# Sixteen-head attentions: scores computed twice, four heads at a time, in place of transposed probabilities

## The chip, the cores and the metric

The kernel runs as one program on one core of a Trainium2 chip. The metric is the device time of one execution in microseconds; three runs of the kernel before gave 1425.77, 1425.83 and 1428.66 us. The engines of the core have short names in what follows: PE multiplies matrices, and the loading of its stationary operand has a row of its own, PEld; DVE, ACT and POOL work on tiles element by element; SP issues transfers (DMA). SBUF is the memory in which tiles lie, PSUM the small memory of eight banks that PE writes its products to, 512 float32 numbers in each of 128 partitions to a bank.

## The reference, cut to what matters

A decoder of two layers works on x of 8 batches x 256 tokens x 256 features, all in float32. After each of six sublayers the input is added and the sum normalised. The sublayers are a state-space mixer, a cross-attention, a mixture of experts, a self-attention with rotated queries and keys, a second cross-attention, and a self-attention whose tokens are split in two sets. Only the fourth and the sixth are touched. Both have 16 heads of 16 features.

```python
def _L1_attn_ref(x, w_qkv, w_out, b_out):          # "rotary"
    q, k, v = ...                                   # 16 heads of 16
    q = _apply_rope(q, cos, sin); k = _apply_rope(k, cos, sin)
    attn = softmax(einsum('bhsd,bhtd->bhst', q, k) * SCALE)
    out = einsum('bhst,bhtd->bhsd', attn, v)
    return einsum('bsd,ed->bse', out, w_out) + b_out

def _L1_ffn_ref(x, g_info, W_qkv, W_proj, b_proj):  # "split"
    pos = sim > 0.9                 # a sign for each token, from its normed queries
    def masked_attn(tok_mask):      # keys: 5 registers and the tokens of one sign
        l = where(key_mask, q * scale @ k, -inf)
        return softmax(l) @ v
    reg_out = (x_pos[:, :REG] + x_neg[:, :REG]) * 0.5
    tok_out = where(pos, x_pos[:, REG:], x_neg[:, REG:])
    return concatenate([reg_out, tok_out]) @ W_proj + b_proj
```

So a query of 256 tokens sees 256 keys; in the split attention only those of its own sign, and the registers attend twice.

## The kernel before

Both attentions use one class, `Heads16`, which runs them in 32 steps, four to a batch. The class `Rotary` and the function `split` give it queries, keys and a term to add, and the work that stands between its parts.

Queries and keys lie feature by token: a partition is a feature, and 32 partitions hold a pair of heads. The keys exist in two copies, each with one head of the pair set to zero (`kps`, made by POOL with the constant `slot`, L1189 and L1391). So a matmul over 32 partitions gives one head's scores, and both copies side by side give two heads' scores in 512 columns.

Step i has half of the heads, c, and one block of 128 queries, qb. `scores` (L1023) makes four matmuls, one for each 32 partitions, into two pairs of PSUM banks. A query is a partition here and a key is a column. For each of eight heads DVE adds the term, negates and takes the minimum in one instruction (L1032, 128x256), which also copies the scores to SBUF; ACT takes the exponential with that minimum as its bias and accumulates the sum (L1039).

The products need the keys on the partitions, so `turn` transposes the exponentials of the step before: 16 transposes on PE (L1054) into two pairs of banks, and a copy of each pair to SBUF, one on DVE and one on ACT (L1057). Every second step `products` (L1069) makes 16 matmuls for one c, into the bank "op". The sums are inverted, widened by POOL (L1084), turned by four transposes (L1091), copied (L1096) and multiplied with the products (L1100). `out` is the output projection (L1107).

`work(b, k, place)` puts other work at three places of a step k: projections of the next batch (L988, copied out by DVE or ACT), values (L998), the end of the batch before (normalisation in L104 to L117), and in split the registers (L1430 scores, L1450 turn, L1461 products) and the mask. The term of split is made by POOL and DVE from the signs (L1412, L1415); the signs of batch 0 are spread by a matmul, those of later ones by a DMA from a DRAM tile `sgd` (L1576 writes it, L1408 reads).

A scheduler orders instructions; `issue_after` adds edges that hold an engine's own program order. These put a step's scores first, its `work` and turns after DVE's last minimum was issued. PSUM is divided by tags: three pairs of banks "sc" (scores and turned exponentials), one bank "mm" (all small matmuls), one bank "op".

## Time and profile before

| | us |
|---|---|
| median of three runs | 1425.83 |
| profiled execution, its own time | 1423.73 |
| its span, first to last instruction | 1421.9 |
| rotary attention: first scores start | 711.2 |
| rotary attention: last scores start, last output projection starts | 908.6, 921.5 |
| split attention: first scores start | 1203.9 |
| split attention: last scores start, last output projection starts | 1395.9, 1410.3 |
| busy: PE, DVE, ACT, POOL | 1358.5, 847.1, 651.6, 483.3 |

The two attentions take about 400 us of the 1422. The page gives busy time over the whole program, so a stage has to be read from windows that lie in it, the price of an operation from its group, and the order from the chain of waits. In a timeline row the first number is the start in us, the second the time. A group's row ends with busy us, mean ns of one instruction, and the idle time before them with what ended it. A float32 matmul has two records, each with a weight load of its own. Rows L1032 and L1039 have a second record for the accumulator's reading.

### The profile page before, as it was taken

The numbers are of one execution on the slowest core, as the hardware profiler recorded it, in microseconds if no ns is written. First come the engines' busy times: TensorE is split into PE (matmuls) and PEld (weight loads), VectorE is DVE, ScalarE is ACT, GpSimd is POOL, SyncE is SP. The second block draws the span as 40 slices with busy tenths as digits, with TensorE's granted clock in tenths as the row PEclk, the third lists the DMA queues.
The fourth block names the chain that finished last, engine by engine and source line by source line (L and its number), as shares of the span: only waits on it lengthen the run. The fifth ranks groups of instructions, "written<-read, shape, count | busy, mean of one in ns | idle before, by whom it ended". The sixth has DMA issues, their size and how long they took to land.

```text
span 1421.9 us, 21978 instructions
## 1 busy us (share of the span) xinstructions
PE 1358.5 (96%) x7946; PEld 947.0 (67%) x7946; DVE 847.1 (60%) x2306; ACT 651.6 (46%) x1612; POOL 483.3 (34%) x510
## 2 busy tenths in 40 slices
PE   8999999999999999999989999999999999899996
PEld 3455678888866666656656666577878777666554
DVE  3776465555643223324578888745556563887885
ACT  3455533333331022221178787643332323867884
POOL 0100012131200132236346666332334454465541
PEclk9999999999999999999999999999999999999999
DMA  8000053335240022242120000025231200000100
GB/s 279 3 1 0 1 161 95 105 91 162 93 192 0 24 74 89 79 142 66 34 82 2 1 1 1 1 86 161 75 95 60 90 7 9 16 16 24 24 16 16
DMA packets 71487, 87.97 MB, mean 62 GB/s; under 512 B 5588, under 2 KB 66164, under 8 KB 70868
## 3 DMA queue, kind: packets, MB, share of 16 engines
q1 hardware_dynamic: 67972, 77.26, 17.0%
q0 software_dynamic: 3408, 9.31, 2.3%
q8 instruction: 64, 1.05, 0.3%
q14 instruction: 43, 0.35, 0.1%
HBM read 57.03 MB, written 29.52 MB: 61 GB/s over the span
## 4 chain that ended last, share of the span: by engine, by line
PE 65%; DVE 12%; POOL 3%; issue 2%; ACT 2%; DMA 1%; POOLq 0%; DVEq 0%; ACTq 0%; SPq 0%
PE mm L521 9%; PE sc L476 8%; PE mm L779 7%; DVE p L1032 6%; PE mm L842 5%; PE op L1069 4%; PE ps_sc L1054 4%; PE ps_sc L1023 4%; PE tr L796 4%; PE tr L856 2%; PE sc L505 2%; PE sc L457 2%; PE sc L411 2%; PE sc L375 2%; PE ps_mm L988 1%
## 5 line engine op out<-in xcount | busy, mean ns | idle before, releaser
L1039 ACT ACTIVATE p<-p,nmx 128x256 f32<-128x256 f32 x512 | 252.9, 496 | 65.2 <-DVE nmx L1032 65.1
L496 POOL TENSOR_TENSOR p<-p,sm 128x616 f32<-128x616 f32 x60 | 72.7, 1217 | 245.1 <-DVE sm L493 218.5
L521 PE MATMUL mm<-Ub,pT 128*128 128x256 f32 (+1 forms) x640 | 144.6, 379 | 0.5 <-ACT pT L75 0.4
L476 PE MATMUL sc<-M,xT_s 128*128 128x308 f32 x512 | 139.0, 423 | 1.1 <-ACT pT L75 1.1
L1054 PE MATMUL ps_sc<-ident,p 128*128 128x128 f32 x1024 | 133.3, 278 | 6.5 <-DVE nmx L1032 4.8
L1054 PEld LDWEIGHTS ps_sc<-ident,p 128*128 128x128 f32 x1024 | 114.6, 142 | 33.3 <-issue 13.3
L521 PEld LDWEIGHTS mm<-Ub,pT 128*128 128x128 f32 (+1 forms) x640 | 120.8, 190 | 20.0 <-ACT pT L75 0.9
L476 PEld LDWEIGHTS sc<-M,xT_s 128*128 128x128 f32 x512 | 94.4, 188 | 35.3 <-ACT pT L75 2.1
L489 ACT ACTIVATE p<-p 128x616 f32<-128x616 f32 x64 | 45.9, 717 | 154.4 <-DVE p L485 132.7
L779 PE MATMUL mm<-xT_s,w 128*128 128x512 f32 x256 | 113.4, 595 | 2.2 <-DVE h L785 2.2
L1032 DVE CUSTOM_DVE_ANT_0 p<-ps_sc,zero 128x256 f32<-128x256 f32 x256 | 90.7, 421 | 27.3 <-PE ps_sc L1023 25.7
L1032 DVE CUSTOM_DVE_ANT_0 p<-ps_sc,term 128x256 f32<-128x256 f32 x256 | 90.7, 419 | 25.8 <-PE ps_sc L1023 25.7
L1039 ACT ACTIVATION_READ_ACCUMULATOR p<-p,nmx 128x1 f32 x512 | 95.9, 187 | 0.0
L816 POOL DMA_INDIRECT xb<-xd,token x39 | 37.3, 956 | 146.2 <-PE tr L823 81.0
L779 PEld LDWEIGHTS mm<-xT_s,w 128*128 128x128 f32 x256 | 47.8, 190 | 56.0 <-issue 52.6
L1057 DVE COPY pT<-ps_sc 128x1024 f32<-128x1024 f32 x64 | 77.6, 1213 | 3.0 <-PE ps_sc L1054 3.0
L483 DVE TENSOR_REDUCE nmx<-sc 128x8 f32<-128x616 f32 x64 | 51.1, 798 | 46.2 <-PE sc L476 46.2
L1057 ACT COPY pT<-ps_sc 128x1024 f32<-128x1024 f32 x64 | 63.7, 996 | 26.8 <-PE ps_sc L1054 26.7
L842 PE MATMUL mm<-wE,xbT 128*128 x156 | 73.5, 593 | 0.3 <-ACT xbT L828 0.3
L783 ACT ACTIVATE g<-mm 128x512 f32<-128x512 f32 x32 | 19.1, 597 | 100.8 <-PE mm L779 99.7
L492 DVE TENSOR_REDUCE sm<-p 128x8 f32<-128x616 f32 x64 | 50.6, 790 | 22.2 <-ACT p L489 21.8
L114 POOL TENSOR_SCALAR rstd<-mv 128x2 f32<-128x2 f32 x48 | 10.8, 225 | 155.2 <-DVE mv L112 154.6
(295 smaller groups left out, 2635.7 us busy)
## 6 DMA issues: line engine op xcount, KB each, us to landing
Ub<-ud SPq DMA_DIRECT2D x32, 512.0 KB
ud<-U SPq DMA_DIRECT2D x16, 616.0 KB
wE<-in_wE SPq DMA_DIRECT2D x4, 1536.0 KB
yd<-y SPq DMA_DIRECT2D x39, 128.0 KB
Ub<-ud SPq DMA_DIRECT2D x32, 104.0 KB
ud<-U SPq DMA_DIRECT2D x4, 608.0 KB
x_s<-in_x SPq DMA_DIRECT2D x8, 256.0 KB
w<-in_Wo SPq DMA_DIRECT2D x2, 1024.0 KB
```

The source lines that it names most:

```text
L476: nc.tensor.matmul(sc[:, a, : 4 * NCTX], xT_b[:, kc, j * P : (j + 1) * P], M[:, a * 4 : a * 4 + 4, kc, at : at + NCTX], start=kc == 0, sto ...
L496: engine.tensor_tensor(pv, pv, bcast(sm, 2, [P, 8, NCTX]), ALU.mult)
L521: nc.tensor.matmul(o[:, j * D : (j + 1) * D], pT[:n, c, j * P : (j + 1) * P],  Us[b][:n, g, c], start=g == 0 and j == 0 and c == 0, stop=g ...
L779: nc.tensor.matmul(ps, w[:, kc, cols], xT_s[:, kc, :], start=kc == 0, stop=kc == 1)
L796: nc.tensor.matmul(o[:, j * D : (j + 1) * D], hs[c][:, at : at + P], w3[:, c, :], start=c == 0, stop=c == 7,)
L842: nc.tensor.matmul(ps, xT[:, kc, :], column(j, kc * 512, 512), start=kc == 0, stop=kc == 1)
L1023: self.last_score = nc.tensor.matmul(scs[s // 2][:, s % 2, :], self.queries(b, c, s, qb), self.keys(b, c, s), start=True, stop=True, tile_ ...
L1032: self.last = nc.vector.tensor_tensor_reduce(out=p[:, h, :], in0=s4[:, h, :], in1=self.term(b, qb), scale=-1.0, scalar=3.0e38, op0=ALU.add ...
L1039: nc.scalar.activation(p[:, h, :], p[:, h, :], AF.Exp, bias=nmx[:, qb, n : n + 1], scale=-1.0, accum_out=sums[:, qb, n : n + 1],)
L1054: nc.tensor.transpose(tr[:, at : at + P], p[:, h, kb * P : (kb + 1) * P], ident)
L1057: (nc.scalar.copy if j else nc.vector.tensor_copy)(self.pT[b, c, j][:, :, :, qb * P : (qb + 1) * P], tr.rearrange("p (h k t) -> p h k t", ...
L1069: nc.tensor.matmul(self.op[b][s * 32 : (s + 1) * 32, c, :], va[:, kb, 8 * c + 2 * s + m, :], self.pT[b, c, s // 2][:, s % 2 * 2 + m, kb, : ...
```

## The change

A step now has four heads and all 256 queries, and computes their scores twice. All in `Heads16`:

- `scores` makes eight matmuls with 256 columns, the queries of both blocks against one copy of the keys. DVE takes plain maxima, four at a time in 128x1024 (L1038 of the changed kernel), negated, into one column in 32 of a tile that is zero elsewhere; the scores are not copied.
- `turn_maxima` turns that tile with two transposes (L1048): the maxima come out as one row in every 32 partitions. `shifted` adds them to the queries (rotary in one instruction with a mask, L1188; split L1403). The keys hold ones in that row, a feature of the other head's that is not used.
- `exponentials`, one step later, makes the scores again with the keys as the stationary operand (L1061), so that they come out turned and shifted, and ACT takes exponentials from PSUM straight to the tile that the products read (L1069, 128x1024).
- `products`, two steps later, makes eight matmuls (L1080). The values' tile has ones in its unused columns, so the sums come out with the products. ACT copies them to SBUF (L1087).
- The sums go by DMA to a packed tile (L1091, 64 pieces of 64 bytes), are inverted (L1098), go back by two DMAs (L1100), are spread over partitions by a shuffle (L1108), and multiplied (L1112), after a predicated copy that merges the two heads of a pair (L1109).

In split the mask is no longer a term added by DVE. Two rows of each 32 partitions hold the signs, marked by DMAs from `sgd` into queries and keys (`marked`, eight a batch), and the queries exist in two copies. The bank "op" is now handed out by `side()` for products, turned maxima, turned outputs and the registers' matmuls. Projections, values and output projections are split in halves (`halves`) that stand before and after the second scores, and their copies are on ACT. What was `work` is a table of events by step and place.

```diff
         def scores(self, i):
-            c, qb = divmod(k, 2)
+            c, m = divmod(k, 2)
             scs = [self.pair() for _ in range(2)]
-            for s in range(4):
-                self.last_score = nc.tensor.matmul(
-                    scs[s // 2][:, s % 2, :], self.queries(b, c, s, qb), self.keys(b, c, s),
-                    start=True, stop=True, tile_position=(s * 32, 0),
+            for qb in range(2):
+                for s in range(4):
+                    nc.tensor.matmul(
+                        scs[s // 2][:, s % 2, qb * SEQ : (qb + 1) * SEQ],
+                        self.queries(b, c, s, m)[:, qb * P : (qb + 1) * P],
+                        self.keys(b, c, s, m), start=True, stop=True, tile_position=(s * 32, 0),
+                    )
+            for j in range(2):
+                self.last = nc.vector.tensor_reduce(
+                    self.mx[m][:, :, 2 * j : 2 * j + 2, self.free[m]].rearrange("p q s -> p s q"),
+                    scs[j].rearrange("p s (q t) -> p s q t", q=2), AX.X, ALU.max, negate=True,
                 )
...
+        def turn_maxima(self, i):
+            ps = self.side()
+            for qb in range(2):
+                nc.tensor.transpose(
+                    ps[:, qb * P : (qb + 1) * P],
+                    self.mx[m][:, qb].rearrange("p s x -> p (s x)"), ident,
+                )
+            qs = self.qs[i] = self.c2.tile([P, SEQ], F32, tag="qs", name="qs")
+            self.shifted(b, c, m, qs, ps[:, :SEQ])
+
+        def exponentials(self, i):
+            scs, qs = [self.pair() for _ in range(2)], self.qs.pop(i)
+            for kb in range(2):
+                for s in range(4):
+                    nc.tensor.matmul(
+                        scs[s // 2][:, s % 2, kb * SEQ : (kb + 1) * SEQ],
+                        self.keys(b, c, s, m)[:, kb * P : (kb + 1) * P],
+                        qs[s * 32 : (s + 1) * 32], start=True, stop=True,
+                        tile_position=(s * 32, 0),
+                    )
+            pT = self.pT[i] = self.c2.tile([P, 4, 2, SEQ], F32, tag="pT", name="pT")
             for j in range(2):
...
+                last = nc.scalar.activation(
+                    pT[:, 2 * j : 2 * j + 2].rearrange("p s k t -> p s (k t)"), scs[j], AF.Exp
+                )
...
         def run
-                with tc.issue_after(self.last.ins), tc.issue_after(self.last_score.ins):
-                    work(b, k, 0)
-                    if 0 <= i - 1 < n:
-                        self.turn(i - 1, 0)
-                    work(b, k, 1)
-                    if i % 2 and 0 <= i - 2 < n:
-                        self.products((i - 2) // 4, (i - 2) // 2 % 2)
-                    if 0 <= i - 1 < n:
-                        self.turn(i - 1, 1)
-                    work(b, k, 2)
...
+                with tc.issue_after(self.last.ins):
+                    if 0 <= i - 2 < n:
+                        bound(self.products, i - 2)
+                    for f in events.get((i, 0), ()):
+                        bound(f)
+                    with ExitStack() as st:
+                        if 0 <= i - 1 < n:
+                            st.enter_context(
+                                tc.issue_after(bound(self.exponentials, i - 1).ins)
+                            )
+                        for f in [*events.get((i, 1), ()), *events.get((i, 2), ())]:
+                            bound(f)
+                        if i < n:
+                            bound(self.turn_maxima, i)
+                        for f in events.get((i, 3), ()):
+                            f()
...
     class Rotary:
+            for b in range(NB):
+                t = 4 * b
+                for c in range(2):
+                    put(t + 4 + 2 * c, 3, at.inverted, b, c)
+                    put(t + 5 + 2 * c, 3, at.normed, b, c)
+                put(t + 7, 3, biased, b)
+                o = t + (10 if b < NB - 1 else 8)
+                halves(o, lambda b, ps, h: at.out(at.oT[b], self.W[2], ps, h), b)
+                emptied(o, added, b)
+                put(o + 1, 3, finish, b)
+                if b < NB - 1:
+                    put(o + 2, 2, lambda b: turn_out(b, at.side(), nc.vector.tensor_copy), b)
```

`bound` keeps PE's work in this order, and events of place 3 are free of it. With t the batch's first step, split has the same table for outputs, and for registers: scores at t, turn at t+2, products at t+3.

## The prediction

> **What bounds the kernel now.** The span is 1421.9 us and the profiled execution took 1423.73 us, 2.1 us below the median of the three runs, 1425.83 us. I make the sum against 1423.73 us and add 2.1 us at the end. About 0.2% (2.9 us) is what a measurement can tell from no change.

> I read the windows view first, over one steady batch of each kind: rotary, split with the projections of a later batch, split without them. Columns: busy us (count) of PE, PEld, DVE, ACT, POOL; granted clock; DMA share; GB/s.

> ```profile
> 760.00:786.00 26.00, 25.00 (x205) 17.36 (x204) 22.46 (x86) 20.79 (x71) 16.77 (x17) 1.00 0.01 2
> 1221.00:1249.00 28.00, 26.18 (x212) 17.89 (x210) 23.39 (x94) 22.75 (x81) 12.83 (x16) 1.00 0.06 11
> 1353.00:1377.00 24.00, 22.40 (x194) 14.03 (x190) 20.64 (x84) 20.36 (x73) 9.46 (x14) 1.00 0.04 12
> ```

> PE is busy 25.0 of 26, 26.2 of 28 and 22.4 of 24 us at full clock: in the first two PE is the bound, and DVE and ACT are not far behind. In the third DVE shares it. Next, the chain of waits through the rotary batch (start, us, what):

> ```profile
> 789.32 1.14 PE ps_sc L1023 x8
> ...
> 794.24 1.99 PE ps_mm L988 x8
> 796.23 1.07 PE ps_sc L1023 x8
> 797.30 0.59 PE ps_mm L1091 x4
> 797.89 0.87 PE ps_sc L1054 x8
> 798.77 1.86 PE op L1069 x32
> 800.63 1.02 PE ps_sc L1054 x8
> 801.65 1.08 PE ps_sc L1023 x6
> ```

> Apart from one stretch at DVE (790.46 to 794.24, left out here: maxima, then the copy that frees the projection's bank), PE goes from piece to piece with no gap, so PE time taken out of a batch is time gained until something else binds. From the chain's L1069 pieces (760.74, 786.42, 812.12) a rotary batch takes 25.7 us; a split batch takes 28.1 us (1221.13 to 1249.17) or 23.8 (1329.06 to 1352.87). Last, what each kind of instruction costs: groups (page and a window), and single rows of the timeline (start, us, engine).

> ```profile
> L1039 ACT ACTIVATE p<-p,nmx 128x256 f32<-128x256 f32 x512 | 252.9, 496 | 65.2 <-DVE nmx L1032 65.1
> L483 DVE TENSOR_REDUCE nmx<-sc 128x8 f32<-128x616 f32 x64 | 51.1, 798 | 46.2 <-PE sc L476 46.2
> L1057 DVE COPY pT<-ps_sc 128x1024 f32<-128x1024 f32 x64 | 77.6, 1213 | 3.0 <-PE ps_sc L1054 3.0
> L1057 ACT COPY pT<-ps_sc 128x1024 f32<-128x1024 f32 x64 | 63.7, 996 | 26.8 <-PE ps_sc L1054 26.7
> ```

> ```profile
> 789.24 0.31 PEld L1023 LDWEIGHTS ps_sc<-kp,qr 32*128 32x128 f32 x8 [0.17 <-issue]
> 789.25 1.14 PE L1023 MATMUL ps_sc<-kp,qr 32*128 32x512 f32 x8
> 790.31 1.59 PEld L988 LDWEIGHTS ps_mm<-xT_s,w 128*128 128x128 f32 x8 [0.76 <-issue]
> ```

> ```profile
> 1198.29 0.31 SPq L1576 DMA_DIRECT2D sgd<-sgT  x1
> 1201.53 7.19 SPq L1408 DMA_DIRECT2D rows<-sgd  x2
> ```

> **The change part by part.** A step is a quarter of a batch; there are 32 steps in each of the two attentions.

> *PE of a step.* Removed: 16 transposes, which the chain shows as 1.02 + 0.87 to 1.03, about 1.95 us, and per batch the four of L1091 (0.59). Kept: products, 1.86 us (32 records) for two steps, 0.935 each. Kept in work, but cut in two: the score pass. One of 4 matmuls with 512 columns takes 1.07; now 8 with 256 columns. Added: a second such pass, and two transposes (0.25, at 0.122 each). A pass of half-width matmuls has no row here. Below: the products' pace, 8 records of 256 columns per 0.468 us on four tiles at once, 0.94 us a pass. Above: each of the doubled groups pays the overhead over that pace again, 1.07 + 0.13 = 1.20. I take 1.07. A step then needs 1.07 + 0.935 + 1.07 + 0.25 = 3.33 us of PE against 1.07 + 1.95 + 0.935 = 3.95.

> *The weight loads* are what speaks against this. A step has 8 loads of 128 columns for scores before and 32 after. At the row's 182 ns each, end to end, 16 would make a pass of 2.9 us; but 8 lie in a stretch of 0.31 us, so the four row groups load side by side, and 16 fit in 0.62, under a pass of 1.07. I put them at nothing; their cover is the streaming itself. [...] The row of 8 in 0.31 us shows 39 ns a load, so here I go by the row.

> *DVE of a step.* Removed: 8 of L1032 at a pitch of 0.345 (2.76 us) and a 1.21 us copy. Added: two maxima of 128x1024. From L483, 798 ns for 616 columns, at the 1.04 ns a column between it and the 420 ns of 256 columns, 1.22 us each; and the shifted queries, 128x256, 0.41 as similar rows. 2.85 against 3.97. Per batch, two reciprocals (0.2), two shuffles (half of 0.73), two predicated copies and two products (0.41 each) replace reciprocal, copy and product (0.35, 0.69, 0.68): about 1 us more. Two projection copies (0.64, 0.69) go to ACT. DVE falls from 22.4 to some 18 a rotary batch.

> *ACT.* Eight exponentials with their accumulator reads at a pitch of 0.495 (3.95) and a copy of 1.0 become two of 128x1024 at about 1.02 and a copy of 128x256 at 0.375: 2.4 against 4.95, so from 20 to 11.5 a batch with three 0.59 us copies.

> *New waits.* The work that leaves PE is not all gained. (a) Maxima, turn, shift, second scores and exponentials are one chain. Behind the turned maxima PE holds the next scores, and behind the shift DVE holds the next maxima. Four pairs of banks a step rotate through three buffers. Half of a pass runs after its buffer comes free before the first maxima or exponentials can start: 0.53 + 0.1 + 1.22 + 0.2 + 0.53 + 0.1 + 1.02 + 0.2 = 3.9 us from one release to the next, 4.85 if the whole pass must end first. A step with projections needs 3.33 + 1.9 = 5.23 on PE, so there the ring is hidden; a split step without them has a ring of 3.9 to 4.85, not 3.33. I take 4.4. (b) One bank, "op", now serves products, turned maxima, turned output and the registers' three products. Each extra user must be read before PE goes on: 0.5 of PE, 0.3 of handing over and 0.69 of copying for an output, 1.5 in all; half of that for the smaller reads of the registers. (c) DVE runs in order, and the shift stands behind the events of its step. Up to about 2 us of them fit while PE does its second pass, and the fourth step has more (statistics 1.2, normalisation 1.2): 1.0 a batch.

> *Sums.* Rotary, steady: 4 x 5.23 + 1.5 + 1.0 = 23.4 against 25.7. The first batch, with four extra pieces in the side bank, takes 25.7; the second, without outputs, 21; the third 22.4; the last, without projections, 20.6. First to last scores: 183.3 less the last step's 5.2, 178 us against 197.4 (711.2 to 908.6): -19. Split: with projections, 4 x 5.23 + three register pieces (1.0, 0.65, 1.25 of PE and waiting) + 1.0 + 0.5 = 25.3 against 28.1; without, 3 x 4.4 + 5.23 + the same 4.4, and 0.7 for events that no longer fit under so short a step, 23.5 against 23.8; the first two, with fewer outputs behind them, 20 and 20.7. First to last scores: 20 + 20.7 + 3 x 25.3 + 3 x 23.5 less the last step's 5.2, 182 against 192.0 (1203.9 to 1395.9): -10.

> *The ends.* The divisor's way now has two DMA hops (the products' sums to a packed tile, their inverses back) in place of a POOL copy and four transposes. A hop is 0.35 of issue and, by the wait of 2.8 us for sgd, some 3.15; the second issues two, 3.5. Last scores to last output projection: maxima, turn, shift 4.6, second pass and exponentials 3.5, products and copy 1.4, hops and reciprocal 6.9, normalisation 1.5: 17.9 against 12.9 in rotary (908.6 to 921.5, +5) and 14.4 in split (1395.9 to 1410.3, +3.5). At the split's start eight marks are written from sgd, 0.36 us of SP each, and must land before the first scores: 1201.5 + 2.9 + 2.8, 1207.2 and the weights' wait, against 1203.9: +4. POOL loses the terms of L1412 and L1415 and the copy of L1084; it bounds nothing. SP gains 8 DMAs a batch (2.8 us), and 9 more in split (3.2): it is nowhere near full.

> Sum: -19 - 10 + 5 + 3.5 + 4 = -16.5, so 1407.2 in the profiled execution and 1409 in the median.

> **The rivals.**

> *A. The PE sums come out clean.* For it: the chain shows no gaps at PE for loads, and half-width passes may run at 0.94. Then 4 x 4.97 + 0.5 = 20.4 for a rotary batch (-5.3 x 7), 4 x 4.97 + 2 = 21.9 for a split one with projections (-6.2 x 3) and 3 x 3.9 + 4.97 + 2 = 18.7 without (-5.1 x 5); with the ends, +12.5, that is -68: 1358. Halfway from mine is 1383. Against: a single bank for four users.

> *B. The DMA hops end last; slower.* In split steps of 4.4 us a pair of sums is copied 2.4 us into a step, lands at 2.4 + 3.15 and is read after the next step's maxima, at 4.4 + 3.0: some 2.0 to spare. The inverses go out 3.3 us into their step, land at 6.8 and are read at 7.4: some 0.5 to spare. DVE would stand at the shuffle, and behind it the shift and PE's second pass. SP issues in order, and a finished output, or marks that wait for POOL's keys, stand ahead. If a hop takes as long as the waits for Ub (5.0) and not 2.8, then 16 inverses wait 1.7 each, 16 sums 0.2 and four hops at the ends 2.2: 27 + 3 + 9 = 39, so 1448. It outweighs my gain of 16.5 from 1.2 us more a hop (16 x 0.7 + 4 x 1.2). Against: sgd's landing, beside few other transfers.

> *C. Weight loads lengthen both passes.* If they overlap only two and two, 16 x 0.182 / 2 = 1.46 us a pass, +0.39 x 128 = 50, so 1459. Against: the row of eight loads in 0.31.

> *D. The change does less than it says:* the gain is eaten and the time stays within 0.2%; a point between mine and B.

> **How the numbers follow.** Mine 0.43 (its own range 1392 to 1426, from passes of 0.94 to 1.20, which move 64 steps by -0.13 x 2 and +0.13 x 2, -17 and +17). A 0.24, B 0.18, C 0.10, D 0.05. Faster: mine and A, 0.67; same, D, 0.05; slower, B and C, 0.28. The range takes in the nearer two thirds of A and B to its price: 1374 to 1448; beyond it lie C and the end of A, 0.18.

> **What would show it.** Right: the second pass (L1061) at 1.0 to 1.1 us beside a first pass (L1032) of the same; maxima (L1038) at 1.2; a rotary period of 22 to 24 us with PE at most 90% busy, and PE waiting for DVE at the turned maxima (L1048). A: PE over 95% busy and periods near 20.5. B: DVE idle before the shuffle (L1108) or the reciprocal (L1098), released by DMA. C: PEld over 0.8 us in a pass, and passes above 1.3. Wrong altogether if another place than the two attentions moves by more than 3 us, or if the clock granted falls below 0.97 in them.

## The result, and the profile after

The changed kernel takes 1420.99 us (median of 13 runs, 1418.06 to 1424.42) against 1426.41 us (13 runs) of the kernel before: a ratio of 0.996, 95% interval 0.9949 to 0.9972, or 5.4 us less. The forecast was 1409 us, 16.5 us less. The sign and the range hold; two thirds of the gain are missing.

The profiled execution of the changed kernel took 1418.84 us, its span 1417.1. Four lines of two pages: the granted tensor clock in 40 slices, of the kernel before and of the changed one, then two groups of the changed kernel (busy us, mean ns of one, idle time before):

```profile
PEclk9999999999999999999999999999999999999999
PEclk9999999999999999999999999999999998999996
L1038 DVE TENSOR_REDUCE mx<-ps_sc 128x4 f32<-128x1024 f32 x128 | 150.8, 1221 | 39.2 <-PE ps_sc L1032 39.1
L1069 ACT ACTIVATE pT<-ps_sc 128x1024 f32<-128x1024 f32 x128 | 124.1, 1021 | 97.0 <-PE ps_sc L1061 97.0
```

The new operations cost what was expected of them: 1.221 us for four maxima (1.22), 1.021 us for four exponentials (1.02). What is new is the clock: the 34th slice has an 8 and the last one a 6, where the kernel before has 9 throughout.

The windows view of the changed kernel over one batch each of rotary, split with projections, and split without (columns as before):

```profile
787.20:810.70 23.50, 22.71 (x241) 14.54 (x240) 17.17 (x32) 10.68 (x15) 14.67 (x15) 1.00 0.02 3
1270.50:1296.70 26.20, 24.31 (x247) 15.27 (x246) 17.70 (x35) 11.34 (x17) 8.39 (x12) 1.00 0.07 20
1321.30:1345.30 24.00, 21.02 (x227) 12.56 (x226) 17.05 (x35) 9.48 (x15) 8.40 (x12) 0.93 0.08 21
```

A rotary batch takes 23.4 us instead of 25.7, a split batch with projections 26.2 instead of 28.1, and the one without that is shown 24.0 instead of 23.8, at a clock of 0.93 (the one ahead of it takes 22.7). The chain of waits of the changed kernel through the longest rotary step shows where PE still stands:

```profile
803.79 1.07 PE ps_sc L1032 x16
804.87 1.00 PE op L1080 x16
805.87 1.06 PE ps_mm L1005 x4
806.93 1.08 PE ps_sc L1061 x16
808.01 1.06 PE ps_mm L1005 x4
809.07 0.45 PE op L89 x4
...
809.54 0.70 DVE xT_s L94
...
810.29 0.44 PE op L1048 x2
810.73 1.07 PE ps_sc L1032 x16
```

Both score passes take 1.07 to 1.08 us. PE has no gap but at the turned output, L89, whose copy must leave the shared bank before the maxima are turned: this step takes 6.94 us, its neighbours 5.49.

Where the time went, in stretches of the two profiled executions (us; starts from the chain and the timeline):

| stretch | before | after | change | forecast |
|---|---|---|---|---|
| start to the first rotary scores | 711.2 | 711.9 | +0.7 | 0 |
| first to last rotary scores | 197.4 | 177.4 | -20.0 | -19 |
| last rotary scores to the cross-attention's first L457 | 24.4 | 30.3 | +5.9 | +5 |
| L457 to the copy of the signs (sgT) | 265.0 | 270.6 | +5.6 | 0 |
| sgT to the first split scores | 6.0 | 6.9 | +0.9 | +4 |
| first to last split scores | 192.0 | 183.5 | -8.5 | -10 |
| last split scores to the last output projection | 14.4 | 23.2 | +8.8 | +3.5 |
| output projection to the end of the span | 11.6 | 13.4 | +1.8 | 0 |

Taken whole, the two stretches of scores came out as reckoned within 1.5 us; that the split one did so by errors that cancel is shown further on. What is missing by this table lies between and behind them.

### The profile page after: what moved, and what is told of

It reads as the page before. It is cut to its first block, busy times and chain, and to the rows that moved or that the text cites. A ratio compares the mean times of both kernels' runs of the same rounds, so it can differ in the third digit from the quotient of the medians.

```text
span 1417.1 us, 21778 instructions
## 1 busy us (share of the span) xinstructions
PE 1337.2 (94%) x8518; PEld 916.2 (65%) x8518; DVE 784.0 (55%) x1505; ACT 490.9 (35%) x734; POOL 423.7 (30%) x470
## 4 chain that ended last, share of the span: by engine, by line
PE 71%; DVE 6%; POOL 3%; issue 2%; DMA 2%; ACT 1%; SPq 0%; another core or an unknown queue 0%; POOLq 0%; DVEq 0%; ACTq 0%
PE mm L521 9%; PE sc L476 8%; PE mm L779 7%; PE ps_sc L1032 5%; PE mm L842 5%; PE ps_sc L1061 5%; PE op L1080 4%; PE tr L796 3%; PE ps_mm L1117 3%; PE ps_mm L1005 3%; PE tr L856 2%; PE sc L505 2%; PE sc L375 2%; PE sc L457 2%; PE sc L411 2%
## 5 line engine op out<-in xcount | busy, mean ns | idle before, releaser
L1038 DVE TENSOR_REDUCE mx<-ps_sc 128x4 f32<-128x1024 f32 x128 | 150.8, 1221 | 39.2 <-PE ps_sc L1032 39.1
L1069 ACT ACTIVATE pT<-ps_sc 128x1024 f32<-128x1024 f32 x128 | 124.1, 1021 | 97.0 <-PE ps_sc L1061 97.0
L476 PE MATMUL sc<-M,xT_s 128*128 128x308 f32 x512 | 138.9, 423 | 1.1 <-ACT pT L75 1.1
L476 PEld LDWEIGHTS sc<-M,xT_s 128*128 128x128 f32 x512 | 94.4, 188 | 35.3 <-ACT pT L75 2.1
L1061 PE MATMUL ps_sc<-qs,kp 32*128 32x256 f32 x1024 | 82.9, 411 | 0.6 <-DVE mx L1038 0.6
L1080 PE MATMUL op<-pT,va 128*32 128x256 f32 x1024 | 74.4, 405 | 5.0 <-DVE qs L1188 2.2
L483 DVE TENSOR_REDUCE nmx<-sc 128x8 f32<-128x616 f32 x64 | 51.1, 799 | 46.2 <-PE sc L476 46.2
L1061 PEld LDWEIGHTS ps_sc<-qs,kp 32*128 32x128 f32 x1024 | 52.9, 189 | 28.4 <-issue 23.9
L492 DVE TENSOR_REDUCE sm<-p 128x8 f32<-128x616 f32 x64 | 50.6, 790 | 22.2 <-ACT p L489 21.9
L1087 ACT COPY o<-op 128x256 f32<-128x256 f32 x64 | 23.8, 372 | 111.7 <-PE op L1080 111.7
L181 PE MATMUL pair<-xT_s,w 128*128 128x512 f32 x128 | 57.9, 612 | 0.9 <-DMA w<-in_W_inT 0.9
L254 PE MATMUL pair<-xc,w 128*128 128x512 f32 x128 | 58.6, 600 | 0.0
L828 DVE COPY hT<-tr 128x256 f32<-128x256 f32 x39 | 16.6, 425 | 75.7 <-PE tr L823 75.7
```

What stands on the lines that cost most here:

```text
L181: last = nc.tensor.matmul(ps[:, i, :], w_in[:, kc, c * P : (c + 1) * P], xT_s[:, kc, :], start=kc == 0, stop=kc == 1,)
L254: last = nc.tensor.matmul(ps[:, i, :], w_dt[:, kc, c * P : (c + 1) * P], xc[s][kc // 2][:, kc % 2, :], start=kc == 0, stop=kc == 3,)
L476: nc.tensor.matmul(sc[:, a, : 4 * NCTX], xT_b[:, kc, j * P : (j + 1) * P], M[:, a * 4 : a * 4 + 4, kc, at : at + NCTX], start=kc == 0, sto ...
L1038: self.last = nc.vector.tensor_reduce(self.mx[m][:, :, 2 * j : 2 * j + 2, self.free[m]].rearrange("p q s -> p s q"), scs[j].rearrange("p s ...
L1061: nc.tensor.matmul(scs[s // 2][:, s % 2, kb * SEQ : (kb + 1) * SEQ], self.keys(b, c, s, m)[:, kb * P : (kb + 1) * P], qs[s * 32 : (s + 1) ...
L1069: last = nc.scalar.activation(pT[:, 2 * j : 2 * j + 2].rearrange("p s k t -> p s (k t)"), scs[j], AF.Exp)
```

## The experiments

All ratios are to the kernel before, from runs on the same chip; "of the changed kernel" compares with its 0.996, an uncertainty of some 2 to 4 us.

### One attention at a time

Two kernels carry both versions of `Heads16`, each attention using one of them. In outline:

```diff
     class Heads16:      # as changed
+    class Heads16Old:   # as before
...
-    rotary / split as changed, both
+    one of them as before, on Heads16Old
```

> Rotary attention changed, split attention left as it was. Pieces (profile after against before): the rotary scores' stretch 20.0 us shorter, its drain up to the cross-attention's first work 5.9 longer, its start 0.7 later, so -13.4 us for the rotary half. Theory 1 (the two halves add up): about 1412.5 us, ratio 0.9905. Rival (the next cross-attention and the signs hide what the drain moves): -19 or more (1407), or only the net -5 seen for both halves (1421).

> Split attention changed, rotary left as it was. Theory 1: the preparation ahead of the split scores costs +6.5, its scores' stretch gains 8.5, its drain and end lose 10.5, so +8.5 us: 1434 us, ratio 1.006. Rival (the split half gains as forecast, -2.5, and what was lost belongs to the rotary half's knock-on): 1423 us or less.

Measured: rotary alone 0.987 (0.9854 to 0.9885), -18.6 us, and split alone 1.0071 (1.0057 to 1.0085), +10.1 us. The sum, -8.5, is near the -5.4 of both together. Rotary's half gained more than its stretches showed (-13.4), near the rival's number, and more than the -14 forecast for it (-19 + 5). Where the extra came from isn't shown: the execution that was profiled took 1413.17 us, only 10.6 less than that of the kernel before. Split's half is a loss, 12.6 us worse than the -2.5 forecast (-10 + 3.5 + 4). The error is in the split half.

### The early copy behind the signs' chain

Rows of the changed kernel's timeline, in the stretch before the split scores:

```profile
1168.94 5.44 POOL L1357 TENSOR_TENSOR ssq<-ssq,nhalf 128x32 f32<-128x32 f32 x1
1174.41 0.42 DVE L1365 TENSOR_TENSOR dot<-dot,ssq 128x256 f32<-128x256 f32 x1 [6.00 <-POOL ssq L1357]
1175.44 0.75 DVE L1438 TENSOR_SCALAR qm<-ps_sc,cst 128x512 f32<-128x512 f32 x1
1176.24 6.53 PE L1005 MATMUL ps_sc<-xT_s,w 128*128 128x256 f32 x16 [3.93 <-DVE qm L1438]
1189.52 0.38 PE L1645 MATMUL ps_mm<-ident,sg 128*32 128x128 f32 x2
```

The change makes two copies of each batch's queries, the second on DVE (L1438). On DVE a product stands ahead of that copy and waits for POOL, with DVE idle for 6.00 us. The copy holds its PSUM pair, PE stands for 3.93 us, and the next 16 records take 6.53 us instead of 3.62 (the same kind in the run below): the granted clock is at half from 1175.15 to 1181.97. The transposes of the signs (L1645) stand behind them on PE.

```diff
+                if first:
+                    nc.scalar.activation(
+                        qms[b][:, 1], v, AF.Identity, scale=cs["scaled"][:, 1:2]
+                    )
+                    return
                 nc.vector.tensor_scalar(
                     qms[b][:, 1], v, cs["scaled"][:, 1:2], None, ALU.mult
                 )
```

`first` is set for the five batches projected ahead of the scores.

> The changed kernel, but the masked second copy of the early queries (L1438, five batches ahead of the split scores) is made by ACT instead of DVE. Theory 1 (DVE's copy stands behind the signs' chain, which waits 5.4 us for POOL, keeps its PSUM pair, and PE stands 3.9 us and then runs slow): the signs' transposes come about 6 us earlier and the whole is 5 to 6 us shorter than the changed kernel, 1415 us, ratio 0.992. Rival (the signs' chain through POOL and DVE sets the start of the scores by itself): no difference, 1421 us.

Measured: 0.9908 (0.9894 to 0.9922), 7.4 us less than the changed kernel. The timeline of this run:

```profile
1171.89 3.62 PE L1005 MATMUL ps_sc<-xT_s,w 128*128 128x256 f32 x16
1175.35 1.89 PE L1014 MATMUL ps_sc<-w,xT_s 128*128 128x256 f32 x8
1182.25 0.38 PE L1650 MATMUL ps_mm<-ident,sg 128*32 128x128 f32 x2
```

PE goes on without a stop, and the signs are turned at 1182.25 instead of 1189.52. The theory holds.

### The registers in the shared bank

The timeline of the changed kernel, a step of a split batch without projections:

```profile
1336.08 1.10 PE L1530 MATMUL op<-pn,vn 128*128 128x64 f32 x8
1337.62 0.43 DVE L1112 TENSOR_TENSOR oT<-o,wide 128x256 f32<-128x256 f32 x1
1338.17 0.28 DVE L1535 TENSOR_TENSOR od<-op,cst 128x128 f32<-128x128 f32 x1
1338.51 0.44 PE L1048 MATMUL op<-ident,mx 128*128 128x128 f32 x2 [1.33 <-DVE od L1535]
1338.88 2.04 PE L1032 MATMUL ps_sc<-kp,qm 32*128 32x256 f32 x16
```

The registers' products (L1530) are written to the bank that the turned maxima need next, and their reading (L1535) stands behind the normalisation in DVE's queue. So PE waits not for a read of 0.28 us but for the queue ahead of it: 1.33 us. The scores that follow take 2.04 us instead of 1.15, at a granted clock of 0.50 (1339.0 to 1342.4).

```diff
-                qd, sc = rg[b], at.side()
+                qd, sc = rg[b], (at.side if 1 < b < 5 else at.mm)()
...
-                pn, vn, on = rg.pop(b), vns.pop(b), at.side()
+                pn, vn, on = rg.pop(b), vns.pop(b), (at.side if 1 < b < 5 else at.mm)()
```

> The changed kernel, but the registers' scores and products of five of eight batches go to the bank of the small matmuls, which is free there, instead of the bank that the products and turned maxima share. Theory 1 (the shared bank costs split steps what PE waits for nsl and od at L1048, 11.3 us in all, 7 in these five batches): 5 to 7 us less, 1415 us, ratio 0.992. Rival (the split steps without projections are set by DVE's row of work, the wait only shows it): 0 to -2, 1420 us.

Measured: 0.9864 (0.9846 to 0.9882), 13.7 us less than the changed kernel, twice what was expected. The same step in this run:

```profile
1332.68 1.10 PE L1530 MATMUL ps_mm<-pn,vn 128*128 128x64 f32 x8
1333.62 0.39 PE L1048 MATMUL op<-ident,mx 128*128 128x128 f32 x2
1333.94 1.15 PE L1032 MATMUL ps_sc<-kp,qm 32*128 32x256 f32 x16
1334.77 0.28 DVE L1535 TENSOR_TENSOR od<-ps_mm,cst 128x128 f32<-128x128 f32 x1
```

The maxima are turned ahead of the reading, the next scores take 1.15 us at a granted clock of 1.00 (1332.7 to 1336.1), and this batch takes 20.5 us (first scores at 1313.40 and 1333.94) instead of 22.7, the next 21.4 instead of 24.0. Of the 13.1 us between the two profiled spans, 8.5 lie between the first and the last split scores and 4.1 behind them, up to the last output projection. The waits seen at PE, 7 us in the five batches, were about half; the rest came with what followed them, such as the scores at half clock (2.04 us). The two parts were not separated.

### Order of the last step

```diff
+                        late = i == n - 1
+                        with tc.issue_after(self.newest(mybir.EngineType.DVE)) if late else nullcontext():
                             for f in events.get((i, 3), ()):
                                 f()
```

> The changed kernel, but in the last step of each attention the other work of DVE (statistics, normalisation, reciprocal, 2.3 us) is issued after the shift of the queries instead of ahead of it. Theory 1 (PE waits for DVE's queue at the last turned maxima, and the clock halves in that gap): 2 us gained in each drain and the slow clock shorter, 1421 - 4 to -8, that is 1413 to 1417 us. Rival (the drain is set by the two DMA hops behind it, or the normalisation now comes late): no gain, 1420 to 1422 us.

Measured: 0.9947 (0.9932 to 0.9962), 1.9 us less than the changed kernel, within the uncertainty. The chain of waits in this run's rotary drain:

```profile
898.60 2.69 POOL x_s L117 x2
...
901.33 0.92 PE op L89 x3
...
903.11 1.93 PE op L1080 x16
```

What was put behind the shift is the statistics that POOL's normalisation waits for; the turned output (L89) waits for that, and the next products wait for its bank. In these profiled executions the rotary drain takes 33.5 us instead of 30.3, and the split drain, where no turned output follows, 19.3 instead of 23.2. So the queue ahead of the shift does cost the split drain something, and the same order costs the rotary drain nearly as much. As a whole the theory fell.

### Unread matmuls in the drains

In the changed kernel's drains PE stands for up to 5.3 us at a time (from 1398.4), and matmuls beside these gaps run at half speed: the sixteen records of products take 1.93 us there (1387.91) and 1.07 at full clock (1322.35), and on the two drains' chains such differences make some 8 us (an estimate from the chain's pieces). A filler of matmuls that nobody reads keeps PE busy there.

```diff
+        def fill_in(self, w, x, count, ps):
+            for k in range(count):
+                nc.tensor.matmul(ps[:, :SEQ], w[:, 0, :P], x[:, 0, :], start=True, stop=True)
...
+            last = 4 * NB - 1
+            put(last, 2, lambda: at.fill_in(wqkv, xT_of(NB - 1), 6, at.mm()))
+            put(last + 1, 2, lambda: at.fill_in(wqkv, xT_of(NB - 1), 4, at.mm()))
+            put(last + 4, 2, lambda: at.fill_in(wqkv, xT_of(NB - 1), 20, at.side()))
```

This is split's part; rotary has 10 and 12 in the same way.

> The changed kernel with matmuls that nobody reads (128x256, in a free bank) put where PE stands in the last steps: rotary 10 ahead of the last turned maxima and 12 ahead of the last output projection, split 6, 4 and 20. Nothing else is moved, and the work added fits into the gaps (2.1 to 5.3 us each). [...] Rival (the drains are set by DVE, POOL and the DMA hops, and PE's speed there is hidden): 1421 us or, by the work added, up to 1426.

> Rotary attention changed, split as it was, and the unread matmuls of the rotary drain (10 and 12). Theory 1: the half-clock windows of the rotary drain cost 2.4 us on its chain: 2 to 3 us less than the rotary change alone, ratio 0.985. Rival: no gain, 0.987 or more.

> The changed kernel with the early copy on ACT, the registers' matmuls of five batches in the other bank, the unread matmuls in both drains, and 9 and 6 more around the first split scores, where PE waits for the marks. Theory 1: -7.4 (measured for the copy) - 8 (drains) - 5 (a halved clock over 13.7 us at the split's start) - 5 (bank): 1396 us, ratio 0.979, faster than the rotary change alone (0.987). Rival (only the copy counts): 1414 us, 0.991.

Measured: 0.9992 (0.998 to 1.0003), 0.9896 (0.988 to 0.9913) and 0.9914 (0.99 to 0.9928): each slower than its like without filler (0.996, 0.987, and 0.9835 below). But the filler was too large. I had read the four records of half a projection (1.06 us) as four matmuls; they are two. From the chain of the first of these runs, the 20 matmuls, 0.43 us each:

```profile
1404.68 1.92 PE ps_mm L1117 x8
1406.60 8.63 PE op L1124 x40
1415.24 1.74 PE ps_mm L1117 x8
```

They ran past the gap and delayed the last output projection. So the three runs don't tell what the clock costs. Again, with some 0.4 of the number:

> As the run with unread matmuls in the drains, with fewer: rotary 4 and 7, split 2, 2 and 8. The first try reckoned a matmul of 128x256 at 0.265 us; the traces show 0.53 (two records), so that its 20 overran their gap (8.6 us). These take 2.1 and 3.7, 1.1, 1.1 and 4.2 us at full clock. Theory 1 (halved clock in the drains costs some 8 us): 1413 us, 0.990. Rival (the drains are set by DVE, POOL and DMA, the matmuls' slowness is hidden, or lost again because the clock is halved when the filling starts): 0.996 to 0.998, 1421 to 1424 us.

Measured: 0.9912 (0.9889 to 0.9935), 6.8 us less than the changed kernel, give or take some 4. The chain of waits in the split drain, first of the changed kernel, then of this run:

```profile
1380.60 1.09 PE ps_sc L1032 x16
...
1387.35 0.43 DVE qs L1403
...
1387.91 1.93 PE op L1080 x16
1389.85 2.09 PE ps_sc L1061 x16
...
1393.04 2.83 PE op L1080 x16
1395.87 2.52 PE ps_mm L1117 x8
...
1403.72 3.72 PE ps_mm L1117 x8
```

```profile
1377.64 1.09 PE ps_sc L1032 x16
...
1384.19 0.43 DVE qs L1410
...
1384.76 1.07 PE op L1080 x16
1385.83 1.15 PE ps_sc L1061 x16
...
1388.99 1.06 PE op L1080 x12
1390.05 1.94 PE ps_mm L1117 x8
...
1397.31 1.98 PE ps_mm L1117 x8
```

The same matmuls take 1.07, 1.15 and 1.98 us instead of 1.93, 2.09 and 3.72. From the last split scores to the last output projection it takes 19.7 us instead of 23.2, from there to the end 1.8 less, and from the last rotary scores to L457 27.3 instead of 30.3: 8.3 us in this execution, 6.8 in the timed runs. The clock granted between the last scores and L457 is 1.00 instead of 0.89, and in the split drain 1.00 instead of 0.71. So the halved clock accounts for most of what the drains and the end lost beyond the forecast (0.9, 5.3 and 1.8 us).

### Do the losses add up

> The changed kernel with the early copy on ACT and the registers' matmuls of five batches in the other bank, and no unread matmuls. Theory 1 (the two are different losses and add up): -7.4 and -13.7 from 0.996, 0.981, about 1400 us. Rival (the split stage has one limit, and either edit reaches it): 0.986, 1406 us.

> The changed kernel, but rotary's turned outputs of batches 0 to 5 go to the bank of the small matmuls, one step later, right after the first scores, with their copy on ACT under the products. Theory 1 (the shared bank costs 1.45 us a rotary batch, the step of 6.94 us beside 5.49, of which the 0.45 of PE stays): 6 x 1.0 = 6 us less, 1415 us, 0.992. Rival (the step's length is set by DVE's row of work and the copies only stand in it): 0 to -2 us, 0.995 to 0.996.

> The changed kernel with the early copy on ACT, the registers' matmuls of five batches and rotary's turned outputs of six batches in the other bank. Theory 1 (all three add up): 0.996 less 0.0052, 0.0096 and 0.0042, that is 0.977, 1394 us. Rival (rotary gains nothing by its part): 0.981.

The edit to rotary's turned outputs:

```diff
                     bound(self.scores, i)
+                for f in events.get((i, -1), ()):
+                    bound(f)
...
-                if b < NB - 1:
+                if b < NB - 2:
+                    put(o + 3, -1, lambda b: turn_out(b, at.mm()), b)
+                elif b < NB - 1:
                     put(o + 2, 2, lambda b: turn_out(b, at.side(), nc.vector.tensor_copy), b)
```

Measured: the copy and the registers together 0.9835 (0.9813 to 0.9858), 17.8 us less than the changed kernel where the single runs add up to 21.1, within the uncertainty: two losses that are separate for the most part. The turned outputs alone 0.9938 (0.9913 to 0.9962), 3.1 us less where 6 were expected, unclear by itself; in its chain the step that holds L89 goes from 6.94 to 6.42 us and rotary's batch from 23.4 to 22.9 (794.18 to 817.12). All three: 0.9803 (0.9783 to 0.9822), 1398.35 us, faster than either kernel.

What was still open was the first split batch, which takes 20.6 us in the changed kernel (20 forecast) but 22.3 with the early copy alone, and whether a clock kept at full adds to the best version:

> The changed kernel with the early copy on ACT, and 5 and 3 unread matmuls (2.6 and 1.6 us) before the first split scores and before their turned maxima, where PE waits for the marks. Theory 1 (the idle 3 us there halve the clock for 13.7 us, which stretches the first steps): 3 to 5 us less than the copy alone, 0.9880. Rival (the marks' transfers and POOL's keys set these steps): 0.990 to 0.992.

> All three edits of the best version so far and the unread matmuls in both drains (4 and 7; 2, 2 and 8) and at the split's start (5 and 3). Theory 1 (a clock kept at full saves what it saved on the changed kernel, 6.8 us, and 3 at the start): 0.9803 - 0.007, 0.9735, 1388 us. Rival (with the other losses gone the gaps are shorter and the unread matmuls overrun them): 0.980 or more.

Measured: 0.9905 (0.989 to 0.992) and 0.9792 (0.9779 to 0.9805). Neither differs clearly from the same kernel without filler (0.9908 and 0.9803). In the profiled execution of the first, the passes at half speed at the split's start are gone (the first products take 1.07 us, 1.94 in the run with the early copy alone) and the first four steps take 18.5 us instead of 22.3 (1190.0 to 1208.5; 1190.8 to 1213.1), but the timed runs do not show it. How much of the first batch is clock stays open. In the profiled executions of the best version and of the second run here, the unread matmuls shorten the rotary drain from 31.8 to 27.3 us, while the split scores take 175.3 us instead of 172.3 and the split drain 20.7 instead of 19.1: what they gain in one place they lose in others.

## Why the prediction held in its steps and failed in its sum

The step that failed is "The ends": it priced the drains by durations from full clock, took an idle PE for free, and did not look at what stands ahead of an operation on DVE where no pass of PE covers it. The second step that was mis-sized is the new wait (b). The parts in turn:

**The steps of rotary attention** hold. A pass of half-width matmuls was taken at 1.07 us between 0.94 and 1.20: 1.07 to 1.08. Weight loads were put at nothing: the sixteen of a pass lie in 0.74 us (0.62 reckoned), under the pass. A pass between projections takes 1.07 to 1.08, and rival C falls. Its sign (over 1.3, with loads over 0.8) does appear in 23 of the 121 passes at full clock, which take 1.46 to 1.52 us by the timeline (1.15 for the others, but 1.99 for the first) with loads over 1.05 to 1.12, most of them in split steps without projections. In one of these the second half of the pass starts 0.38 us after the first (1323.35 and 1323.74), 0.06 us after the first of the maxima ended (1323.68), which points to the ring (a) and not to the loads. A steady rotary batch was put at 23.4 and takes 23.4, but by terms that make up for each other: half projections take 1.06 and products 1.00 (0.95 and 0.935 reckoned), so that a step is 5.49 and not 5.23; the shared bank's turned output costs 1.45 (1.5); and DVE's surplus in the fourth step (1.0) costs nothing.

**The DMA hops, rival B,** fall too. In the drains a transfer takes 1.7 us from the start of its issue (0.56 us on the queue) to the end of the wait for it, and the pair that carries the inverses 2.3, not 3.15 and 3.5. Between the first and last rotary scores no engine's wait is put down to them; they show in the drains.

**The new wait (b), the shared bank,** was right as a mechanism and mis-sized in split. It was taken as a matmul, a hand-over and a read of its own length. What PE waits for is the whole of DVE's queue ahead of the read, and the registers' scores and products cost some 13.7 us in five batches together with what followed. That the forecast's 23.5 us for a split batch without projections lies between the measured 22.7 and 24.0 is luck: 4.4 us was allowed for the ring (a), and a step with no register matmul behind it takes 4.0 (1321.28 to 1325.30; 1317.88 to 1321.90 with the registers in the other bank). The ring's upper bound of 4.85 would be 4.98 by its own terms, which changes nothing.

**What was not in the sum** is the failed step. "The ends" priced the drains at durations from full clock and the preparation by the marks alone. Three things were missed there.

First, L1438: the change adds a second copy of the queries on DVE, and I listed the copies that ACT takes over but not what stands ahead of this one on DVE. It cost the 5.6 us of the stretch from L457 to sgT (7.4 by its run).

Second, the clock. The drains and the end were put at +5, +3.5 and 0 and took +5.9, +8.8 and +1.8. With PE kept busy there, 6.8 us came back. An idle PE was counted as time at no price.

Third, DVE's queue in the drains. By the terms of the sum, and in the order of the chain above, the split drain was to take 4.6 (maxima, turn, shift), 3.5 (second pass, exponentials), 1.4 (products, copy) and 8.4 us (hops, reciprocal, normalisation). It takes 7.2, 5.2, 2.9 and 7.9; with the unread matmuls 7.0, 4.3, 1.1 and 7.3. So the two middle terms were short mostly because of the clock (4.9 us reckoned, 8.1 taken, 5.4 at full clock). The first stays long at full clock: some 2.5 us of other work stand ahead of the shift on DVE, which (c) counts in a steady step but not in the last one. In rotary the forecast of +5 came near +5.9 by luck: with the unread matmuls it is +2.9, so terms priced too high, the hops for one, stood in for the clock.

Of the signs that were set, two of being wrong altogether came: another place, L457 to sgT, moved by 5.6 us, and the granted clock is 0.93 from the first split scores to the last output projection (1.00 in the rotary scores). Of the signs of being right, the passes, the maxima and the rotary period of 23.4 came, but not "PE at most 90% busy" beside that period: PE is busy for 95% of the rotary scores' stretch (93% before). In the split one it is 90% (92% before).

By the stretches, measured less forecast: +0.7 at the start (which lies between 709.6 and 712.8 in the profiled runs of changed kernels), -1.0 and +0.9 in rotary and its drain, +5.6 up to the signs, -3.1 for marks that cost less than thought, +1.5 in the split scores, +5.3 and +1.8 behind them. That is +11.7, from -16.5 to the -4.8 between the two spans. The +1.5 is a balance: the shared bank and the clock cost there (the registers' run gained 8.5 in that stretch), and the steps by themselves are shorter than reckoned.

## What to carry to other kernels

When a change takes work off the engine that bounds a stage, price the gaps that it opens: here PE stood for up to 5.3 us in the split drain, the granted clock there was 0.71, and 6.8 us came back with PE kept busy in both drains. When a scarce buffer gets a second kind of user, look at the queue that its reader stands in, not at the read alone: here a wait of 1.33 us for a read of 0.28. And of each instruction that is new on an engine, look up what is already queued there, in the quiet stretches before and behind the loop too.

## What the runs showed of the hardware

```profile
1332.20:1335.60 3.40, 3.40 (x48) 2.19 (x50) 2.29 (x3) 0.37 (x1) 0.96 (x1) 1.00 0.00 0
1335.60:1339.00 3.40, 2.07 (x22) 1.44 (x19) 3.19 (x13) 1.94 (x2) 1.46 (x3) 1.00 0.01 1
1339.00:1342.40 3.40, 3.40 (x32) 1.68 (x32) 1.88 (x3) 0.00 (x0) 2.92 (x3) 0.50 0.10 33
```

PE is busy for 2.07 of 3.40 us, its one long wait is the 1.33 us for od, and the next window is at half.

The clock also goes with most of the spread between executions of one kernel. Over 85 executions of the changed kernel and the experiments, each taken against its own kernel's mean, time falls by 8.4 us for each 0.01 of mean clock (correlation -0.91). The kernel before runs at 0.991 (mean of 40), the changed one at 0.974 to 0.980. At that slope the difference would be worth some 12 us, about what the forecast was short by. That is an estimate: it carries a slope found within kernels over to a difference between two, and it holds the clock's part of the losses above once more. With unread matmuls it does not carry over: the best version with them runs at 0.993 instead of 0.987, which would be worth 5 us, and its ratio is 0.9792 instead of 0.9803, 1.6 us.
